# Attention outputs turned in two half-array products, divided on GpSimd, with the instruction order picked from fifteen plans

## The chip, the core and the metric

The kernel runs on one core of a Trainium2 chip. A core has TensorE (PE; its weight loads are shown apart, as PEld), VectorE (DVE), ScalarE (ACT), GpSimd (POOL) and SyncE (SP), which here only issues transfers. Each engine takes its instructions in the order in which they stand in its own queue; semaphores order the engines among each other. The metric is the time of one execution on the device in microseconds (us). Matrix products land in PSUM, which the kernel manages as eight banks of 128 x 512 float32.

## The reference

A stack of two transformer layers over 2048 tokens of 256 features, each an attention with 16 heads of 16 features and a gated feed-forward of width 1024; every part adds the layer norm of its output to its input. Cut to what matters:

```python
scores = einsum('bhqd,bhkd->bhqk', q, k) * scale      # causal mask
probs = softmax(scores)                                # over keys
y = einsum('bhqk,bhkd->bhqd', probs, v)
y = y.transpose(0, 2, 1, 3).reshape(B, T, C)
return y @ W_o.T + b_o
...
x = x + layernorm(attn0(layernorm(x)))
x = x + layernorm(ffn0(layernorm(x)))
x = x + layernorm(attn1(layernorm(x)))
x = x + layernorm(ffn1(layernorm(x)))
```

## The kernel before

**Tiling.** The tokens are cut into four chunks `c` of 512, a chunk into four tiles `t` of 128 rows. The heads form four groups `g` of four. One unit of attention is one query chunk with one group of heads; the list `UNITS` names the 16 of a layer in this order: chunk 0 with groups 0 and 1, chunks 1, 2 and 3 with all four groups, chunk 0 with groups 2 and 3. The keys of a unit run over tiles `kt` up to the end of its own chunk.

**One unit.** First come the maxima: `maxima` multiplies queries by keys (L749, with the mask added by L745), two halves of the array side by side, a bank each, and DVE takes the largest of every row (L757). The rows of maxima are split into three bfloat16 parts on POOL (L787 to L791), turned by four products with the identity over the whole array (L803), and copied by ACT to `mrow` (L807). Then `weighted` runs over the key tiles: PE adds minus the maximum (L835) and the scores (L840) in two banks, again in halves of the array; ACT takes the exponential (L846) into `pt`; on the tiles of the diagonal POOL zeroes what lies above it (L850); PE multiplies by the values (L857), in four groups of columns of the array, and sums up over the key tiles in one bank, `av`. A value row has 17 columns, the last a one, so that the sum of the exponentials comes along.

**The end of a unit,** which the change touches. ACT copies `av` to `o` (L865); `o` has four heads of 32 rows one below another, and tokens along its columns. The four products of `flip` turn it over the whole array, 128 tokens each, into one bank (L870). `divide` takes the reciprocal of the sums (16 columns: four tiles by four heads, L877) and multiplies (256 columns, L879), both on DVE and straight out of the bank, into `yb[c]`, the attention output of the chunk.

**The end of a chunk.** When its last group is done, `mixed` turns `yb[c]` (L531), multiplies by the output weights (L615), adds the bias (L893), and `add_normed` normalizes and adds it to `x`; the power of -1/2 that the norm needs is taken on POOL (L495, L496). The last chunk to close is chunk 0, at the end of the layer's attention, where the feed-forward follows (L1010, then L1017 to L1022, L976).

**What sets the order.** No order of instructions is written out. A `Plan` collects operations (`plan.op`: engine, an assumed duration, what it reads and writes, a rank), and `Plan.run` plays them through with these durations: it looks for the operation that could start first, and among those of the same engine that could start within `near` of it takes the one of lowest rank, plus `waiting` times its delay. In that order the instructions are emitted, and it is fixed from then on. PE operations carry a mode ("row" for halves of the array, "col" for groups of columns, "full"); a change of mode is priced by `SWITCH`. Banks, and rings of buffers, are handed out in the same play. There are four plans: attention and feed-forward of each layer. In all of them `near` and `waiting` are 0.1.

Of the kernel before, what the change touches and what calls it, by code (L numbers as in the profile page):

```python
# [11 lines left out]
F32 = mybir.dt.float32  # L12
# [5 lines left out]
ALU = mybir.AluOpType  # L18
# [5 lines left out]
DH = 16  # L24
# [6 lines left out]
P = 128  # L31
CH = 512
NCHUNK = T // CH
TPC = CH // P
# [30 lines left out]
class Buf:  # L65


    def __init__(self, make, ring=None, banks=0):
        self.make, self.ring, self.banks = make, ring, banks
        self.tile, self.at = None, ()  # L70
        self.users, self.writers, self.readers = [], [], []
        if ring is not None and banks != 1:
            ring.asked.append(self)
# [8 lines left out]
class Ring:  # L82


    def __init__(self, n, ordered=False):
        self.slots, self.at, self.ordered = [None] * n, 0, ordered
        self.asked, self.given = [], 0


class Banks:  # L90

# [1 line left out]


    def __init__(self, n):
        self.slots, self.asked, self.given, self.limit, self.singles = [None] * n, [], 0, 2, 4

    def ready(self, i):

# [12 lines left out]
    def soonest(self, b, others, later):  # L112


        if b.banks == 2 and (self.asked[self.given] is not b or self.pairs() == self.limit):
            return None
        if later and b.banks == 1:
            used = sum(self.ready(i) is None and self.slots[i].banks == 1 for i in range(len(self.slots)))
            if used + others >= self.singles:
                return None  # L120
        free = sorted(t for t, _ in self.choices(b.banks))
        return free[others] if len(free) > others else None

    def give(self, b, now):
        t, i = min((max(t, now), i if b.banks == 2 else -i) for t, i in self.choices(b.banks))
        b.at = range(abs(i), abs(i) + b.banks)
        for i in b.at:
            self.slots[i] = b
        if b.banks == 2:
            self.given += 1  # L130


class Places:
# [2 lines left out]

    def __init__(self, n, left):
        self.slots, self.asked, self.left = [None] * n, [], left

    def choices(self):  # L140

# [22 lines left out]
class Plan:  # L164
# [7 lines left out]
    free, mode = {}, None  # L172
    LAG = {"DVE": 0.08, "ACT": 0.1, "PE": 0.2}

    def __init__(self, near=0.1, waiting=0.1):
        self.ops, self.near, self.waiting = [], near, waiting

    def op(self, engine, us, fn, r=(), w=(), after=(), hold=(), rank=0.0, mode=None, lanes=(0, 1), lag=0.0, load=LOAD):
        bufs = list(dict.fromkeys([*r, *w, *hold]))
# [13 lines left out]
        self.ops.append(o)  # L193
        return o

    def run(self):
        free, mode, waiting = Plan.free, Plan.mode, {}
        ready, after = [], {}
        for o in self.ops:
            waiting[o] = sum(d.end is None for d in o.after)  # L200
            for d in o.after:
                after.setdefault(d, []).append(o)
            if waiting[o] == 0:
                ready.append(o)
        done = 0
        while ready:
            best = []
            pairs = min((o.rank for o in ready if o.pair and o.pair.tile is None), default=math.inf)
            widest = min((o.rank for o in ready if o.wide and o.wide.tile is None), default=math.inf)
            for o in ready:  # L210
                at = max((d.end + self.HOP for d in o.after), default=0.0)
                wanted = {}
                for b in o.bufs:
                    if b.ring is not None and b.tile is None:
                        ring = b.ring
                        if b.banks:
                            soonest = ring.soonest(b, wanted.get(ring, 0), o.rank > (pairs if b.banks < 3 else widest))
                            wanted[ring] = wanted.get(ring, 0) + 1
                            if soonest is None:
                                at = None  # L220
                                break
                            at = max(at, soonest + self.HOP)
                            continue
                        n = wanted.get(ring, 0)
                        wanted[ring] = n + 1
                        if ring.ordered and ring.asked[ring.given + n] is not b:
                            at = None
                            break
                        old = ring.slots[(ring.at + n) % len(ring.slots)]
                        if old is not None:  # L230
                            if any(u.end is None for u in old.users):
                                at = None
                                break
                            at = max(at, max(u.end for u in old.users) + self.HOP)
                if at is None:
                    continue
                if o.engine == "PE":
                    lanes, more = (o.lanes, 0.0) if o.mode == mode else ((0, 1), self.SWITCH[o.mode] + o.load - self.LOAD)
                    at = max([at + o.load] + [free.get(("PE", x), 0.0) + more for x in lanes])
                else:  # L240
                    at = max(at, free.get(o.engine, 0.0))
                best.append((at, o))
            assert best, "nothing can start"
            first = min(best, key=lambda p: p[0])
            at, o = min((p for p in best if p[1].engine == first[1].engine and p[0] <= first[0] + self.near),
                        key=lambda p: (p[1].rank + self.waiting * (p[0] - first[0]), p[0]))
            for b in o.bufs:
                if b.ring is not None and b.tile is None and b.banks:
                    b.ring.give(b, at)
                elif b.ring is not None and b.tile is None:  # L250
                    b.ring.slots[b.ring.at] = b
                    b.ring.at = (b.ring.at + 1) % len(b.ring.slots)
                    b.ring.given += 1
                b.t
            o.fn()
            if o.engine == "PE":
                mode = o.mode
                for x in (0, 1):
                    free["PE", x] = at + o.us if x in o.lanes else max(at, free.get(("PE", x), 0.0))
            else:  # L260
                free[o.engine] = at + o.us
            o.end = at + o.us + o.lag
            done += 1
            ready.remove(o)
            for n in after.get(o, ()):
                waiting[n] -= 1
                if waiting[n] == 0:
                    ready.append(n)
        assert done == len(self.ops)
        Plan.mode = mode  # L270
        self.span = max(o.end for o in self.ops)


@with_exitstack
def kernel(ctx: ExitStack, tc: tile.TileContext, x_in, cols_in, rows_in, wd_in, wuq_in, rot_in,
# [15 lines left out]
    def new(pool, shape, dtype, tag, name, n, ordered=True):  # L291

        ring = rings.setdefault(tag, Ring(n, ordered))
        assert len(ring.slots) == n
        return Buf(lambda: pool.tile(shape, dtype, tag=tag, name=name, bufs=n), ring)

    def bank(name):
        b = Buf(lambda: psum[:, b.at[0], :], banks, 1)
        return b
# [130 lines left out]

    neghalf = const.tile([P, 2 * TPC], F32, tag="neghalf", name="neghalf")
    nc.gpsimd.memset(neghalf, -0.5)
    ident = const.tile([P, P], F32, tag="ident", name="ident")
    make_identity(nc, ident)

# [254 lines left out]
    class Attention:  # L690
# [28 lines left out]
        def over(self, cs):  # L719

            return [o for c in cs for b in self.kb[c] for o in b.readers]

    rpm, rmx = Ring(2), Ring(2)

    def maxima(layer, plan, n, qb, first_rank, span):
# [84 lines left out]
    def attention(layer, plan, wo, wob, bo, scale, tail):  # L810

        L, Vs, kb, vb = layer.L, layer.V, layer.kb, layer.vb
        with tc.tile_pool(name=f"at{L}", bufs=1) as at:
            yb = {}
            for tag in ("Q", "y", "pt", "o"):
                rings.pop(tag, None)

            def weighted(n, c, g, qb, mrow):
# [44 lines left out]
                rk = n + 1.1  # L863
                o = new(at, [P, CH], F32, "o", f"o{L}{n}", 1)
                plan.op("ACT", 0.50, lambda: nc.scalar.copy(o.t, av.t), r=[av], w=[o], rank=rk)  # L865
                s = bank(f"ot{L}{n}")

                def flip():
                    for t in range(TPC):
                        nc.tensor.transpose(s.t[:, t * P:(t + 1) * P], o.t[:, t * P:(t + 1) * P], ident)  # L870

                plan.op("PE", 0.5, flip, r=[o], w=[s], hold=[yb[c]], rank=rk, mode="full")

                def divide():
                    by = s.t.rearrange("p (n e) -> p n e", e=32)
                    r = small.tile([P, 4 * TPC], F32, tag="r", name=f"r{L}{n}", bufs=4)
                    nc.vector.reciprocal(r, by[:, :, DH])  # L877
                    dst = as_tiles(yb[c].t)[:, :, 64 * g:64 * g + 64].rearrange("p t (j d) -> p t j d", j=4)
                    nc.vector.tensor_tensor(  # L879
                        dst, by.rearrange("p (t j) e -> p t j e", j=4)[:, :, :, 0:DH],  # L880
                        r.rearrange("p (t j) -> p t j", j=4).unsqueeze(3).to_broadcast([P, TPC, 4, DH]), ALU.mult)

                plan.op("DVE", 0.7, divide, r=[s], w=[yb[c]], rank=rk)

            def mixed(c, rank):
                yT = transposed(plan, yb[c], f"y{L}{c}", rank)
# [319 lines left out]
```

## Time and profile before

| | |
|---|---|
| median of three runs | 1311.26 us (1307.37 to 1312.85) |
| the profiled execution, its own time | 1308.48 us |
| its span, first to last instruction | 1306.8 us, mean TensorE clock 0.974 |
| instructions | 22980 |
| L757 on DVE, maxima, 1088 instructions | 672.9 us busy |
| L846 on ACT, exponentials, 640 | 546.0 us busy |
| L865 on ACT, copy of `av` to `o`, 32 | 18.9 us busy, 590 ns each |
| L803 on PE, turning rows of maxima, 128 | 12.9 us busy |
| L531 on PE, turning `y`, 64 | 9.2 us busy |

A line of the profile's groups names the line of the kernel, the engine, the operation, what it writes and reads, the size and the count; then the busy time and the mean duration of one; then the time that the engine stood idle before it, and who ended that. Products on PE overlap, so that 128 of 285 ns can have 20.9 us of busy time. The first attention takes about 80 to 556 us of the span, the first feed-forward about 556 to 690, the second attention 690 to 1188, the second feed-forward the rest.

### The profile page before, as it was taken

To read this page: it belongs to the slowest core of one execution; us is meant where nothing else is said; L and a number is where in the kernel's file an instruction comes from. 1 tells how busy PE (TensorE), PEld (TensorE's weight loads), DVE (VectorE), ACT (ScalarE), POOL (GpSimd) and SP (SyncE) were. 2 spreads that over 40 slices of the span, in tenths; PEclk is the share of its full clock that TensorE was granted. 3 is DMA by queue.
4 is the path that set the end of the run, shared out by engine and by line. 5 is a ranking of instruction groups with operands and counts; after the bars stand their busy time and mean duration, and the time that the engine had idled before them with its cause. 6 is when DMAs were issued, how large, how long until landed. Compare 5 with 4: busy or idle time off the path is not lost.

```text
span 1306.8 us, 22980 instructions
## 1 busy us (share of the span) xinstructions
PE 1218.0 (93%) x8888; PEld 680.9 (52%) x8888; DVE 902.3 (69%) x1714; ACT 795.0 (61%) x1100; POOL 333.4 (26%) x640
## 2 busy tenths in 40 slices
PE   4889999999999999889987999999999999997996
PEld 3655545444444443568765455454444443445884
DVE  4588899889978852364445968978898888234432
ACT  3346654776566678666533566557655676885663
POOL 6032111211110112356422212111101200134564
PEclk8899999999999999989997999999999999998998
DMA  5550501500000000000064041040000000000000
GB/s 152 177 178 17 178 17 40 188 17 18 17 1 18 17 1 18 25 9 1 13 211 137 11 153 42 17 146 17 17 17 18 18 1 17 17 1 2 1 33 33
DMA packets 43488, 65.71 MB, mean 50 GB/s; under 512 B 10740, under 2 KB 15441, under 8 KB 43377
## 3 DMA queue, kind: packets, MB, share of 16 engines
q1 hardware_dynamic: 43040, 63.80, 15.8%
q8 instruction: 70, 1.15, 0.4%
q0 software_dynamic: 48, 0.11, 0.1%
q10 hardware_dynamic: 288, 0.31, 0.1%
q14 instruction: 42, 0.34, 0.1%
HBM read 41.14 MB, written 23.07 MB: 49 GB/s over the span
## 4 chain that ended last, share of the span: by engine, by line
PE 70%; DVE 14%; ACT 4%; DMA 3%; issue 3%; POOL 2%; SPq 2%; POOLq 0%; ACTq 0%; DVEq 0%
PE banks L857 17%; DVE pm L757 12%; PE banks L749 10%; PE banks L835 10%; PE banks L840 8%; PE banks L1010 8%; PE banks L615 7%; PE banks L976 4%; PE banks L745 3%; ACT pt L846 3%; PE banks L531 1%; DMA sc_q<-wide 1%; ACT wide L506 1%; PE banks L870 1%; SPq L567 1%
## 5 line engine op out<-in xcount | busy, mean ns | idle before, releaser
L757 DVE TENSOR_REDUCE pm<-banks 128x1 f32<-128x512 f32 (+1 forms) x1088 | 672.9, 684 | 155.4 <-PE banks L749 150.0
L846 ACT ACTIVATE pt<-banks 128x1024 f32<-128x1024 f32 (+3 forms) x640 | 546.0, 898 | 262.4 <-PE banks L840 242.1
L840 PE MATMUL banks<-Q,K 64*128 64x512 f32 (+3 forms) x1248 | 319.1, 519 | 0.0
L749 PE MATMUL banks<-K,Q 64*128 64x128 f32 (+2 forms) x1728 | 305.1, 359 | 11.1 <-DMA Q<-sc_q 4.9
L857 PE MATMUL banks<-pt,V 128*32 128x512 f32 (+3 forms) x2560 | 303.7, 546 | 1.9 <-POOL pt L850 1.0
L835 PE MATMUL banks<-mrow,sel 64*128 64x512 bf16 (+3 forms) x1280 | 247.5, 354 | 13.0 <-ACT pt L846 8.8
L749 PEld LDWEIGHTS banks<-K,Q 64*128 64x128 f32 x1728 | 193.7, 186 | 111.3 <-DVE pm L757 61.7
L835 PEld LDWEIGHTS <-sel 64*128 64x128 bf16 x1280 | 78.4, 93 | 232.5 <-issue 218.7
L850 POOL TENSOR_SCALAR_AFFINE_SELECT pt<-pt 128x256 f32<-128x256 f32 x256 | 102.7, 406 | 335.5 <-ACT pt L846 332.9
L1010 PE MATMUL banks<-F,F 128*128 128x512 f32 x512 | 134.5, 407 | 5.2 <-DVE wide L557 5.2
L840 PEld LDWEIGHTS banks<-Q,K 64*128 64x128 f32 x1248 | 135.3, 195 | 4.5 <-issue 3.7
L1010 PEld LDWEIGHTS banks<-F,F 128*128 128x128 f32 x512 | 99.2, 196 | 27.3 <-DVE wide L557 5.7
L1019 DVE SCALAR_TENSOR_TENSOR fu<-banks,cols,sl 128x512 f32<-128x512 f32 x64 | 47.4, 750 | 74.3 <-ACT sl L1017 33.1
L857 PEld LDWEIGHTS banks<-pt,V 128*32 128x32 f32 x2560 | 53.0, 108 | 86.5 <-issue 65.5
L1022 POOL TENSOR_TENSOR fl<-fu,fh 128x512 fp32r<-128x512 f32 x64 | 81.7, 1288 | 61.4 <-ACT fh L1021 61.1
L787 POOL TENSOR_SCALAR mx<-best 128x16 bf16<-128x16 f32 x32 | 9.8, 308 | 314.5 <-DVE best L782 314.5
L745 PE MATMUL banks<-mask,half 64*128 64x512 bf16 x256 | 67.3, 388 | 0.3 <-DVE pm L757 0.3
L1021 ACT CAST fh<-fu 128x512 fp32r<-128x512 f32 x64 | 39.5, 621 | 38.6 <-DVE fu L1019 37.2
L976 PE MATMUL banks<-fh,F 128*128 128x512 f32 x128 | 53.0, 414 | 6.6 <-DVE fu L1019 6.6
L976 PE MATMUL banks<-fl,F 128*128 128x512 f32 x128 | 52.3, 408 | 4.4 <-POOL fl L1022 4.4
L1017 ACT ACTIVATE sl<-banks,cols 128x512 f32<-128x512 f32 x64 | 43.5, 689 | 13.7 <-PE banks L1010 13.3
L549 POOL TENSOR_TENSOR x<-x,wide 128x1024 f32<-128x1024 f32 x16 | 37.9, 2371 | 35.0 <-ACT wide L506 35.0
(122 smaller groups left out, 934.1 us busy)
## 6 DMA issues: line engine op xcount, KB each, us to landing
K<-sc_k SPq DMA_DIRECT2D x128, 128.0 KB
Q<-sc_q SPq DMA_DIRECT2D x120, 128.0 KB
sc_q<-wide SPq DMA_DIRECT2D x48, 256.0 KB
sc_k<-wide SPq DMA_DIRECT2D x32, 256.0 KB
x<-in_x_dram SPq DMA_DIRECT2D x4, 512.0 KB
out_dram<-x SPq DMA_DIRECT2D x4, 512.0 KB
f<-in_ffn_dram SPq DMA_DIRECT2D x2, 768.0 KB
F<-sc_q SPq DMA_DIRECT2D x8, 128.0 KB
```

What stands on the lines that cost most here:

```text
L615: nc.tensor.matmul(s.t[:, at:at + n], a, b, start=start, stop=stop)
L745: nc.tensor.matmul(s.t.rearrange("p (d k) -> p d k", k=P), half16[b, x, :], mask_qk[b, x, :, :], start=x == 0, stop=False)
L749: nc.tensor.matmul(s.t[:, to:to + k], qb.t[b, i, t * P:(t + 1) * P], layer.K(kc)[b, 2 * g + i, k0:k0 + k], start=not masked, stop=not mask ...
L757: nc.vector.tensor_reduce(dst, src, AX.X, ALU.max)
L835: nc.tensor.matmul(s.t[:, e, 0:nq], sel[b:b + 64, i, :], mrow.t[b:b + 64, off:CH], start=True, stop=False)
L840: nc.tensor.matmul(s.t[:, e, 0:nq], layer.K(kt // TPC)[b:b + 64, 2 * g + i, k * P:(k + 1) * P], qb.t[b:b + 64, i, off:CH], start=False, st ...
L846: plan.op("ACT", 0.1 + nq / 620, lambda s=s, pt=pt, nq=nq: nc.scalar.activation(pt.t[:, :, 0:nq], s.t[:, :, 0:nq], AF.Exp, scale=scale), r ...
L850: plan.op("POOL", 0.41, lambda pt=pt: nc.gpsimd.affine_select(out=pt.t[:, :, 0:P], in_=pt.t[:, :, 0:P], compare_op=ALU.is_ge, fill=0.0, ba ...
L857: nc.tensor.matmul(av.t[32 * j:32 * j + 32, off:CH], Vs[kt // TPC][:, kt % TPC, DV * h:DV * h + 32], pts[kt, j // 2].t[:, j % 2, 0:nq], st ...
L976: nc.tensor.matmul(dn[dh].t, wdn[:, fc, dh * P:(dh + 1) * P], halves[fc][j].t, start=fc == 0 and j == 0, stop=fc == 7 and j == 1)
L1010: nc.tensor.matmul(s.t[:, i, :], w[:, cc, fc * P:(fc + 1) * P], xT[j].t[:, cc, :], start=n == 0, stop=n == 3)
L1022: plan.op("POOL", 1.3, lambda fu=fu, fh=fh, fl=fl: nc.gpsimd.tensor_tensor(fl.t, fu.t, fh.t.bitcast(F32), ALU.subtract), r=[fu, fh], w=[fl ...
```

## The change

Three things are changed.

1. The output of a unit is turned by a new function, `turned`: for each half `e` of the rows of `o` (two heads, 64 rows) four products with the 64 x 64 identity, into a bank of its own, in mode "row"; and one ACT copy of 256 columns out of each bank into `ot` in SBUF. Eight smaller products and two copies stand where four products stood.
2. The division runs on POOL and reads `ot`: the reciprocal is a power of -1 over 16 columns (`minus1` is a new constant), followed by the multiplication over 256 columns. The plan is given 1.1 us for both.
3. `Plan.run` plays each plan fifteen times, with five values of `near` and three of `waiting`, keeps the pair whose play ends first, and emits that one. The bookkeeping of buffers in the play is rewritten for it (`given`, and `soonest` and `give` of `Ring`) so that a play can be taken back. For this program the four plans take (near, waiting) = (0.05, 0.05), (0.05, 0.05), (0.14, 0.1) and (0.17, 0.05).

The turning of the rows of maxima in `maxima` (L803) is not touched.

```diff
-    def __init__(self, near=0.1, waiting=0.1):
-        self.ops, self.near, self.waiting = [], near, waiting
+    NEAR, WAITING = (0.05, 0.08, 0.11, 0.14, 0.17), (0.05, 0.1, 0.2)
+
+    def __init__(self):
+        self.ops = []
...
-    def run(self):
-        free, mode, waiting = Plan.free, Plan.mode, {}
+    def order(self, near, waiting, emit=False):
...
-            at, o = min((p for p in best if p[1].engine == first[1].engine and p[0] <= first[0] + self.near),
-                        key=lambda p: (p[1].rank + self.waiting * (p[0] - first[0]), p[0]))
+            at, o = min((p for p in best if p[1].engine == first[1].engine and p[0] <= first[0] + near),
+                        key=lambda p: (p[1].rank + waiting * (p[0] - first[0]), p[0]))
...
+    def run(self):
+
+        tried = [(self.order(near, waiting), near, waiting) for near in self.NEAR for waiting in self.WAITING]
+        self.span = self.order(*min(tried)[1:], emit=True)
...
+    minus1 = const.tile([P, TPC, 4, 1], F32, tag="minus1", name="minus1")
+    nc.gpsimd.memset(minus1, -1.0)
...
+    def turned(plan, src, dst, r, w, name, rank):
+
+        for e in range(2):
+            s = bank(f"{name}{e}")
+
+            def flip(s=s, e=e):
+                b = slice(64 * e, 64 * e + 64)
+                for t in range(TPC):
+                    nc.tensor.transpose(s.t[:, t * 64:t * 64 + 64], src(t, b), ident[b, b])
+
+            plan.op("PE", 0.45, flip, r=[r], w=[s], hold=[w], rank=rank, mode="row", lanes=(e,))
+            plan.op("ACT", 0.33, lambda s=s, e=e: nc.scalar.copy(dst(e), s.t[:, 0:TPC * 64].rearrange("p (t q) -> p t q", t=TPC)),
+                    r=[s], w=[w], rank=rank)
...
-                s = bank(f"ot{L}{n}")
-
-                def flip():
-                    for t in range(TPC):
-                        nc.tensor.transpose(s.t[:, t * P:(t + 1) * P], o.t[:, t * P:(t + 1) * P], ident)
-
-                plan.op("PE", 0.5, flip, r=[o], w=[s], hold=[yb[c]], rank=rk, mode="full")
+                ot = new(at, [P, TPC, P], F32, "ot", f"ot{L}{n}", 1)
+                turned(plan, lambda t, b: o.t[b, t * P:(t + 1) * P], lambda e: ot.t[:, :, 64 * e:64 * e + 64], o, ot, f"ot{L}{n}", rk)
 
                 def divide():
-                    by = s.t.rearrange("p (n e) -> p n e", e=32)
-                    r = small.tile([P, 4 * TPC], F32, tag="r", name=f"r{L}{n}", bufs=4)
-                    nc.vector.reciprocal(r, by[:, :, DH])
+                    by = ot.t.rearrange("p t (j e) -> p t j e", e=32)
+                    r = small.tile([P, TPC, 4, 1], F32, tag="r", name=f"r{L}{n}", bufs=4)
+                    nc.gpsimd.tensor_tensor(r, by[:, :, :, DH:DV], minus1, ALU.pow)
                     dst = as_tiles(yb[c].t)[:, :, 64 * g:64 * g + 64].rearrange("p t (j d) -> p t j d", j=4)
-                    nc.vector.tensor_tensor(
-                        dst, by.rearrange("p (t j) e -> p t j e", j=4)[:, :, :, 0:DH],
-                        r.rearrange("p (t j) -> p t j", j=4).unsqueeze(3).to_broadcast([P, TPC, 4, DH]), ALU.mult)
-
-                plan.op("DVE", 0.7, divide, r=[s], w=[yb[c]], rank=rk)
+                    nc.gpsimd.tensor_tensor(dst, by[:, :, :, 0:DH], r.to_broadcast([P, TPC, 4, DH]), ALU.mult)
+
+                plan.op("POOL", 1.1, divide, r=[ot], w=[yb[c]], hold=[yb[c]], rank=rk)
```

## The prediction

> **What bounds the kernel now.** I read the busy shares first, then the same shares by stretch, then the chain of work that ended last, and last the rows of what the change touches. The busy times of the page:
>
> ```profile
> PE 1218.0 (93%) x8888; PEld 680.9 (52%) x8888; DVE 902.3 (69%) x1714; ACT 795.0 (61%) x1100; POOL 333.4 (26%) x640
> PE 70%; DVE 14%; ACT 4%; DMA 3%; issue 3%; POOL 2%; SPq 2%; POOLq 0%; ACTq 0%; DVEq 0%
> ```
>
> The second line is the chain's share by engine: PE carries the end, DVE sometimes takes over, POOL hardly appears. By stretch (PE, PEld, DVE, ACT and POOL busy, clock, DMA), inside the first attention:
>
> ```profile
> 160.00:300.00 140.00, 137.21 (x1117) 68.16 (x1113) 124.45 (x221) 89.54 (x111) 22.79 (x58) 1.00 0.21 65
> 420.00:520.00 100.00, 98.40 (x826) 41.16 (x822) 59.57 (x101) 75.46 (x88) 13.76 (x36) 1.00 0.04 12
> ```
>
> PE is busy 98% in both; beside it DVE has 89% in the early units and ACT 75% in the late ones. POOL has 14 to 16%, at full clock. So a microsecond off PE counts nearly whole, one off DVE in part, one added to ACT little, and one added to POOL nothing unless somebody waits for that instruction. The rows for what is removed or added (mean ns after the count):
>
> ```profile
> L870 PE MATMUL banks<-ident,o 128*128 128x128 f32 x128 | 20.9, 285 | 0.9
> L877 DVE RECIPROCAL r<-banks 128x16 f32<-128x16 f32 x32 | 8.1, 252 | 15.2 <-PE banks L870 13.7 <-ACT pt L846 1.5
> L879 DVE TENSOR_TENSOR y<-banks,r 128x256 f32<-128x256 f32 x32 | 13.6, 425 | 1.1
> L846 ACT ACTIVATE pt<-banks 128x256 f32<-128x256 f32 x64 | 23.0, 386 | 37.5 <-PE banks L840 28.3 <-POOL pt L850 5.0 <-issue 3.5
> L496 POOL TENSOR_TENSOR rs_ya<-ve_ya,neghalf 128x4 f32<-128x4 f32 x8 | 8.3, 1042 | 0.7
> L788 POOL TENSOR_TENSOR rest<-best,mx 128x16 f32<-128x16 f32 x32 | 7.1, 221 | 2.7
> L1022 POOL TENSOR_TENSOR fl<-fu,fh 128x512 fp32r<-128x512 f32 x64 | 81.7, 1288 | 61.4 <-ACT fh L1021 61.1 <-PE banks L1010 0.3
> L549 POOL TENSOR_TENSOR x<-x,wide 128x1024 f32<-128x1024 f32 x16 | 37.9, 2371 | 35.0 <-ACT wide L506 35.0
> ```
>
> The reader is to see one thing above all: L496 is a power of 4 columns and takes 1042 ns; L788 is an addition of 16 columns and takes 221. On POOL a power is not priced like an addition.
>
> **PE, the flips (32 units of head group and query chunk).** In the timeline a flip looks like this:
>
> ```profile
> 322.53 0.18 PEld L749 LDWEIGHTS banks<-K,Q 64*128 64x128 f32 x1 [0.41 <-DVE pm L757]
> 322.95 0.42 PEld L870 LDWEIGHTS banks<-ident,o 128*128 128x128 f32 x4 [0.24 <-ACT pt L846]
> 323.54 0.16 PEld L857 LDWEIGHTS banks<-pt,V 128*32 128x32 f32 x8 [0.17 <-issue]
> ```
>
> The 0.42 us from the last L749 to the first L870 repeats: it is the median of the 21 places where L749 stands before L870, while L749 to a following score product (L835) is 0.16: before it enters the full array PE stands some 0.26 us. The four products start 0.109 apart, and the exit to a score product is 0.205. So a flip between two half-array products takes 0.42 + 3 x 0.109 + 0.205 = 0.95, less the 0.16 that would be there anyway: 0.79 us. After the change each flip is eight products of 64 rows. Nearest row: the eight L749 products 64x128 in two halves, whose first and last start are 0.40 us apart (57 ns each, the two halves side by side). So 0.45 us instead of 0.79: 0.34 saved. Ends: if the loads of the two halves queue at 0.109 each, 0.87 and thus 0.1 lost; if 64 moving columns halve it, 0.55 saved. The built program's order has 28 of 32 flips wholly between half-array products, and entries into full-array mode fall from 81 to 55. 27 x 0.34 = **9 us saved**, ends -15 and +3. Rows of maxima (L803, also full-array, four products each) keep their form: the change's short description names them too, but that half is not in the diff.
>
> **DVE.** Removed: 32 x (252 + 425 ns) = 21.7 us. DVE is on the chain 14% of the time (3 us) and stands at 89% beside a PE that waits for its banks in the early units; I take a third, **7 us saved**, ends 3 and 21.7.
>
> **ACT.** Two copies of 128x256 out of PSUM per unit, priced by the 386 ns row of that size: 32 x 0.77 = 25 us, at 61% busy. In the late units it delays exponentials. With ACT's 4% of the chain it is 1 us, with one in six 4; I take **4 us lost**, ends 0 and 12. Each flip now holds two banks until these copies, where it held one until DVE's division; it is inside these ends.
>
> **POOL, the division.** The multiplication 128x256: from L1022 and L549 the slope is (2371 - 1288) / 512 = 2.1 ns per column and the intercept 0.2, so 0.75 us (estimate from these rows). The reciprocal as a power over 16 columns was never run: if the 1042 ns are fixed, 1.04; if the excess over an addition (1042 - 205 - 8 = 829 ns) goes with columns, 0.2 + 16 x 0.209 = 3.5 us. A rule of the Trainium skill (GPSIMD Engine Reference, section When to use GPSIMD) speaks against the move, but mildly: elementwise work belongs on VectorE, GpSimd takes about twice as long with two inputs. By it the division is estimated at 2 x 0.68 = 1.4 us, near the 1.1 that the planner is given. The row says 1.8 to 4.3. I take 4.3: the planner's own price of the two small instructions at L495/L496 is written as 0.3 + 0.2 per column, the same slope as 0.209. POOL gains 32 x 4.3 = 137 us of work, which fits into its 970 idle; what counts is who waits:
>
> - 24 inner units (chunks 1 to 3, less closings): in POOL's timeline the next instruction after a flip at 322.95 begins at 344.63, and elsewhere 8 to 25 us later. Hidden, 0.
> - Closings: yb of a chunk is turned (L531) after its last group. In the new order four closings in mid-attention have 2.1 to 2.5 us of PE work between flip and y flip. Needed: 0.45 for the flip, 0.2 until readable, 0.77 + half an exponential (0.5) for ACT, 0.1, 4.3 = 6.3 against 0.45 + 2.4: PE, whose queue is in order, stands 3.5 us; four times 14.
> - The two ends of attention: chunk 0 closes and the feed-forward's products stand behind it. Before, in the chain:
>
> ```profile
> 1188.45 0.44 PE banks L870 x4
> 1188.89 1.17 PE banks L1010 x5
> 1190.05 0.45 PE banks L531 x4
> ```
>
>  The wait is covered by L1010. After, one L1010 product stands between: 6.3 - 0.45 - 0.23 = 5.6 us each, 11. Together 25, of which I let a fifth be caught up by engines that run ahead: **20 us lost**. With the rule's 1.4 us it would be 4 x 0.6 + 2 x 2.7 = 8, less a fifth: 6.
> - Chunk 0's units mask every key tile, so L850 stands directly behind the division (0.3 to 0.7 us behind the flip in the trace at units 0, 13 and 14 of each layer). Each then comes up to 4 us later; weighted values and everything behind them in PE's queue wait, with some 2 to 3 us of products as cover: 6 x 1.3 = **8 us lost**, ends 0 and 15; 1 by the rule.
>
> **The order.** Each of the four plans is now drawn up fifteen times and the one of least planned span is emitted; it picks (0.05, 0.05), (0.05, 0.05), (0.14, 0.1) and (0.17, 0.05) where (0.1, 0.1) stood. Loads of K and Q on SP's queue change places too, all ahead of use and with 5% DMA share late. No row prices this: between -13 and +10 us, taken as 0. It chooses with the division at 1.1 us, so the covers above are cut to a price which I doubt.
>
> **Sum** by the row: -9 - 7 + 4 + 20 + 8 = +16. By the rule: -9 - 7 + 4 + 6 + 1 = -5. The profiled execution took 1308.48 us (span 1306.8); the median of the runs shown is 1311.26, 2.8 above. 1308.5 + 16 = 1324.5, and I say **1324**.
>
> **Rivals.** *Slower by the power* (the forecast), 0.52: 1324, own range 1314 to 1338; its weak point is that no power over 16 columns was run. It decides where the division on POOL takes over about 2.7 us (half-way between 1.4 and 4.3 the sum passes +5). *Faster*, 0.29: the power costs about the same for 4 and 16 columns, flips save 0.45 us each, and DVE proves to be the brake in the units with 89%, so that half of its relief counts: -12 - 11 + 4 + 6 + 1 = -12, thus 1296, own range 1288 to 1304. For it: the loads of L749 wait 62.7 us for DVE's L757 in the list of waits; against: PE at 98%. *Wash*, 0.13: the division is hidden but so is the gain, 1308 (-5 + 2 of order). *The new order is worse on the chip*, 0.06, whatever the division takes: +12, 1323. [...]
>
> Change smaller than 0.5% (6.6 us) cannot be told from none. Slower by more: 0.42 of the first and all of the last but a little, 0.05, and some of the wash: 0.52, and I give 0.55; same 0.15; faster 0.30. The range 1296 to 1336 leaves about one in ten at each side.
>
> **What would show it.** The power row on POOL at 128x16: 3.5 us right, 1.0 wrong. The multiplication 0.75. PE idle ahead of the turning of y (L531 in the lines of before) at the closings, with POOL's y as the releaser, some 3.5 us each; DVE busy 880, ACT 820, POOL 470. Flips: about 57 ns per product, no 0.42 ahead. If the power takes 1 us and the closings do not stand, the forecast falls and the time is under 1305.

## The result, and the profile after

| | before | after |
|---|---|---|
| median | 1310.97 us (1307.37 to 1312.85, 4 runs) | 1325.41 us (1325.16 to 1327.84, 4 runs) |
| ratio to before, 95% interval | | 1.012 [1.0102, 1.0138] |
| the profiled execution, its own time | 1308.48 us | 1325.32 us |
| its span, mean TensorE clock | 1306.8 us, 0.974 | 1323.6 us, 0.967 |

The changed kernel is 14.4 us slower. The forecast was 1324, by the way that it named the likeliest. New lines are the half flips (L750), their copies (L753), the power (L905) and the multiplication (L907). The others have moved because code was added above them: the turning of `y` is L550 (before L531), the output weights L634 (L615), the mask L883 (L850), the weighted values L890 (L857), maxima L782 and L790 (L749 and L757), the feed-forward's first product L1036 (L1010).

The same two lines of the page of the kernel after, busy times and the chain's shares by engine:

```profile
PE 1220.0 (92%) x9016; PEld 687.4 (52%) x9016; DVE 884.8 (67%) x1650; ACT 809.3 (61%) x1164; POOL 446.8 (34%) x705
PE 68%; DVE 13%; POOL 6%; ACT 5%; issue 3%; DMA 3%; SPq 2%; POOLq 0%; ACTq 0%; DVEq 0%
```

POOL was 2% of the chain and is now 6%: an engine that is idle two thirds of the time has come into the way. PE's busy time has hardly changed (1218.0 before), while the span of the profiled execution grew by 16.8 us: PE stands more. The rows of what was added, by shape (mean ns after the count, then the idle time of the engine before them and who ended it):

```profile
L905 POOL TENSOR_TENSOR r<-ot,minus 128x16 f32<-128x16 f32 x32 | 93.6, 2926 | 150.5 <-ACT ot L753 150.1
L907 POOL TENSOR_TENSOR y<-ot,r 128x256 f32<-128x256 f32 x32 | 19.9, 621 | 2.5
L753 ACT COPY ot<-banks 128x256 f32<-128x256 f32 x64 | 21.8, 395 | 6.7 <-PE banks L750 6.7
L750 PE MATMUL banks<-ident,o 64*128 64x64 f32 x256 | 21.6, 230 | 2.0 <-DVE pm L790 0.5 <-ACT pt L879 0.3 <-DVE wide L671 0.2
L550 PEld LDWEIGHTS banks<-ident,y 128*128 128x128 f32 x64 | 7.1, 146 | 17.4 <-POOL y L907 12.0 <-DVE pm L790 3.0 <-ACT pt L879 1.3
```

The power takes 2926 ns and the multiplication 621: 3.55 us per unit, where DVE took 0.68. And the last line shows who waits for it: the loads for turning `y` stood 12.0 us behind POOL's `y`. The list of waits has that again (total, times, longest), and the masks beside it:

```profile
PEld banks L890 <- POOL pt L883: 14.0, 28, 3.4
PEld banks L550 <- POOL y L907: 12.0, 6, 3.4
PE banks L890 <- POOL pt L883: 6.2, 3, 3.3
```

Before, the first of these was smaller, and in place of the second there was only a short wait for DVE, which divided then:

```profile
PEld banks L857 <- POOL pt L850: 8.2, 27, 1.2
PEld banks L531 <- DVE y L879: 0.8, 2, 0.4
```

The timeline of PE's loads has the six stands one by one (start, length, and in brackets the time that it stood before and for whom):

```profile
226.37 0.42 PEld L550 LDWEIGHTS banks<-ident,y 128*128 128x128 f32 x4 [0.37 <-POOL y L907]
...
560.35 0.72 PEld L550 LDWEIGHTS banks<-ident,y 128*128 128x128 f32 x4 [3.38 <-POOL y L907]
...
853.38 0.42 PEld L550 LDWEIGHTS banks<-ident,y 128*128 128x128 f32 x4 [1.23 <-POOL y L907]
...
1008.20 0.42 PEld L550 LDWEIGHTS banks<-ident,y 128*128 128x128 f32 x4 [1.43 <-POOL y L907]
...
1177.44 0.47 PEld L550 LDWEIGHTS banks<-ident,y 128*128 128x128 f32 x4 [2.25 <-POOL y L907]
...
1207.23 0.42 PEld L550 LDWEIGHTS banks<-ident,y 128*128 128x128 f32 x4 [3.38 <-POOL y L907]
```

Four are closings in mid-attention, with 0.4 to 2.3 us (the other two of the six there show no stand behind POOL); those at 560 and 1207 are the two ends of attention, with 3.4 each. Here is the last one, as the chain of waits tells it (start, length, what):

```profile
1202.09 0.47 PE banks L750 x8
1202.55 0.30 issue
1202.85 0.66 ACT ot L753 x2
1203.51 0.07 issue
1203.58 2.91 POOL r L905
1206.49 0.07 issue
1206.56 0.63 POOL y L907
1207.19 0.04 issue
1207.24 0.65 PE banks L550 x4
1207.89 0.43 PE banks L634 x2
1208.33 0.63 PE banks L1036 x2
1208.95 4.54 PE banks L634 x14
```

From the end of the flip (1202.55) to the turning of `y` (1207.24) the chain leaves PE for 4.69 us, of which the power is 2.91. The last line shows a second price: fourteen products of the output weights take 4.54 us here. In the same place before, the chain had

```profile
1192.14 3.04 PE banks L615 x14
```

The stretches (length, busy PE, PEld, DVE, ACT, POOL, granted clock) say why; the first two are those shown of before, inside the first attention, the other two the stand and what follows it:

```profile
160.00:300.00 140.00, 135.81 (x1104) 68.22 (x1101) 115.27 (x202) 87.81 (x116) 41.02 (x69) 0.99 0.20 61
420.00:520.00 100.00, 99.23 (x854) 45.44 (x850) 66.17 (x109) 75.43 (x91) 23.94 (x42) 1.00 0.04 12
1203.00:1208.50 5.50, 2.15 (x13) 1.65 (x13) 0.00 (x0) 1.66 (x4) 3.52 (x2) 1.00 0.00 1
1208.50:1212.00 3.50, 3.50 (x10) 2.81 (x9) 0.38 (x1) 1.98 (x3) 0.00 (x0) 0.52 0.00 0
```

Inner attention is not where the loss is: PE is as full there as before, and DVE's share in the early units has come down from 89 to 82%. After this stand, however, PE runs 3.5 us at half clock.

### The profile page after: what moved, and what is told of

Its sections match the earlier page's. It is cut to its first block, busy times and chain, and to the rows that moved or that the text cites. A ratio compares the mean times of both kernels' runs of the same rounds, so it can differ in the third digit from the quotient of the medians.

```text
span 1323.6 us, 23337 instructions
## 1 busy us (share of the span) xinstructions
PE 1220.0 (92%) x9016; PEld 687.4 (52%) x9016; DVE 884.8 (67%) x1650; ACT 809.3 (61%) x1164; POOL 446.8 (34%) x705
## 4 chain that ended last, share of the span: by engine, by line
PE 68%; DVE 13%; POOL 6%; ACT 5%; issue 3%; DMA 3%; SPq 2%; POOLq 0%; ACTq 0%; DVEq 0%
PE banks L890 17%; DVE pm L790 11%; PE banks L782 10%; PE banks L868 10%; PE banks L873 8%; PE banks L634 7%; PE banks L1036 7%; PE banks L1002 3%; ACT pt L879 3%; PE banks L778 3%; POOL r L905 2%; PE banks L550 1%; ACT wide L525 1%; SPq L586 1%; POOL fl L1048 1%
## 5 line engine op out<-in xcount | busy, mean ns | idle before, releaser
L790 DVE TENSOR_REDUCE pm<-banks 128x1 f32<-128x512 f32 (+1 forms) x1088 | 672.8, 681 | 175.0 <-PE banks L782 172.3
L782 PE MATMUL banks<-K,Q 64*128 64x128 f32 (+2 forms) x1728 | 309.7, 360 | 10.2 <-DMA Q<-sc_q 6.3
L890 PE MATMUL banks<-pt,V 128*32 128x512 f32 (+3 forms) x2560 | 304.3, 545 | 7.9 <-POOL pt L883 6.2
L782 PEld LDWEIGHTS banks<-K,Q 64*128 64x128 f32 x1728 | 197.4, 189 | 85.0 <-DVE pm L790 43.2
L883 POOL TENSOR_SCALAR_AFFINE_SELECT pt<-pt 128x256 f32<-128x256 f32 x256 | 102.4, 406 | 241.4 <-ACT pt L879 239.3
L905 POOL TENSOR_TENSOR r<-ot,minus 128x16 f32<-128x16 f32 x32 | 93.6, 2926 | 150.5 <-ACT ot L753 150.1
L1036 PE MATMUL banks<-F,F 128*128 128x512 f32 x512 | 131.6, 401 | 0.8 <-DVE fu L1045 0.8
L1036 PEld LDWEIGHTS banks<-F,F 128*128 128x128 f32 x512 | 97.0, 191 | 22.0 <-DVE fu L1045 1.2
L890 PEld LDWEIGHTS banks<-pt,V 128*32 128x32 f32 x2560 | 51.9, 108 | 93.5 <-issue 64.8
```

What stands on the lines that cost most here:

```text
L782: nc.tensor.matmul(s.t[:, to:to + k], qb.t[b, i, t * P:(t + 1) * P], layer.K(kc)[b, 2 * g + i, k0:k0 + k], start=not masked, stop=not mask ...
L790: nc.vector.tensor_reduce(dst, src, AX.X, ALU.max)
L883: plan.op("POOL", 0.41, lambda pt=pt: nc.gpsimd.affine_select(out=pt.t[:, :, 0:P], in_=pt.t[:, :, 0:P], compare_op=ALU.is_ge, fill=0.0, ba ...
L890: nc.tensor.matmul(av.t[32 * j:32 * j + 32, off:CH], Vs[kt // TPC][:, kt % TPC, DV * h:DV * h + 32], pts[kt, j // 2].t[:, j % 2, 0:nq], st ...
L905: nc.gpsimd.tensor_tensor(r, by[:, :, :, DH:DV], minus1, ALU.pow)
L1036: nc.tensor.matmul(s.t[:, i, :], w[:, cc, fc * P:(fc + 1) * P], xT[j].t[:, cc, :], start=n == 0, stop=n == 3)
```

## The experiments

My theory: the power on POOL makes the division late at closings and ahead of masks, and PE, whose queue is in order, stands there. Rivals: the half flips with their copies and second bank cost the time; or the new order does, whatever the division takes. Each kernel was timed beside the kernel before (1310.4 to 1311.1 us there); the ratios are to that. "To the letter" below means that `plan.op` is told the same as in the kernel that it is compared with, so that the order of instructions on PE and ACT stays as it was.

### Parts of the change alone

**Division back on DVE**, everything else kept, with the plan told so:

```diff
-  nc.gpsimd.tensor_tensor(r, by[:, :, :, DH:DV], minus1, ALU.pow)
+  nc.vector.reciprocal(r, by[:, :, :, DH:DV])
-  nc.gpsimd.tensor_tensor(dst, ...)
+  nc.vector.tensor_tensor(dst, ...)
-  plan.op("POOL", 1.1, divide, ...)
+  plan.op("DVE", 0.7, divide, ...)
```

> The changed kernel with one part undone: reciprocal and multiplication of the outputs run on VectorE again, now out of the copy in SBUF; the half-array flips, the two copies and the fifteen plans stay. If the division's time in GpSimd's queue behind the closings, the ends and the masks is the cause: 1309 us, from 1303 to 1313. If the new order of instructions is the cause, or the two ScalarE copies and the second bank: 1320 to 1326, no change to the changed kernel.

Measured: 1301.01 us (1300.49 to 1304.49), ratio 0.9934 [0.9918, 0.9949]. 24.4 us below the changed kernel, and below the range that I gave. The division is the loss, and the rest of the change is worth about 9 us, more than either theory gave it. The order is another one here too; the series in one order below separates that.

**The order alone**: the kernel before, with the fifteen plans.

```diff
-  ot = new(at, [P, TPC, P], ...); turned(plan, ...)
+  s = bank(f"ot{L}{n}"); plan.op("PE", 0.5, flip, r=[o], w=[s], ..., mode="full")
-  plan.op("POOL", 1.1, divide, r=[ot], ...)
+  plan.op("DVE", 0.7, divide, r=[s], ...)
```

> The kernel before with the fifteen plans alone; flip over the whole array, division on VectorE out of PSUM. My theory gives the order no part in the loss: 1311 us, from 1305 to 1316. If the order is the cause: 1320 or more.

Measured: 1301.5 us (1300.0 to 1305.08), ratio 0.9936 [0.992, 0.9952]. A miss: the search brings 9 us by itself, and I had put it at nothing. Beside it, the kernel with the division back on DVE shows no gain from the flips: 1301.0 against 1301.5, each in its own order.

**No search**: flips and division as changed, one pair of values.

```diff
-  NEAR, WAITING = (0.05, 0.08, 0.11, 0.14, 0.17), (0.05, 0.1, 0.2)
+  NEAR, WAITING = (0.1,), (0.1,)
```

> The changed kernel with the one pair (0.1, 0.1) of before in place of fifteen: half-array flips and division on GpSimd alone. My theory: as slow as the changed kernel, 1325 us, from 1318 to 1332. If the order is the cause: 1311.

Measured: 1332.14 us (1328.93 to 1335.78), ratio 1.0167 [1.0145, 1.0188]. The search is worth 7 us here too. It hid a third of what the other two parts lose: some 21 us without it, 14 with it.

### The division, unit by unit, in one order

An order drawn anew for each variant moves everything. In the next four kernels the changed kernel's order is kept to the letter, and only the engine that divides is chosen by the number `n` of the unit in `UNITS`:

```diff
+  on_dve = ...
+  if on_dve: nc.vector.reciprocal(r, ...)
+  else: nc.gpsimd.tensor_tensor(r, ..., minus1, ALU.pow)
+  (nc.vector if on_dve else nc.gpsimd).tensor_tensor(dst, ...)
```

**All on DVE** (`True`):

> The changed kernel with its order of instructions kept to the letter (same planner, same prices, same picks); only the engine of the division is VectorE in all 32 units. So the order can't differ. If the division's stay on GpSimd is the cause, this is 1303 us, from 1300 to 1308, and PE no longer waits for y. If the order drawn for the changed kernel is what is bad and the first experiment was fast because its order was another: 1318 or more.

Measured: 1311.2 us (1308.83 to 1314.14), ratio 1.0008 [0.9996, 1.0021]. A miss: between the two cases that I had put down. In one order the division on POOL costs 14.2 us. That is below the 24.4 of the first experiment; the 10 us between the two kernels with the same work come with the order alone, here one drawn without the divisions on DVE, there one drawn with them.

**GpSimd in the inner units alone** (`n in (0, 1, 5, 9, 13, 14, 15)` on DVE):

> The same fixed order; VectorE divides in the units that close a chunk (5, 9, 13, 15) and in those next to masks of chunk 0 (0, 1, 14), GpSimd in the other nine of each layer. The prediction says that these inner units hide the division wholly: no slower than with VectorE everywhere, or up to 3 us faster, as VectorE is relieved of 12 us: 1299 to 1306. If GpSimd's division costs in every unit: 9/16 of the loss, 1313 or more.

Measured: 1305.11 us (1304.24 to 1307.87), ratio 0.9961 [0.9947, 0.9975]. As expected, the slow division is hidden in the nine inner units of a layer. Taking it off DVE gains 6.1 us in this order, twice the most that I had expected; the order reckons with no division on DVE. Its chain at the last closing:

```profile
1186.45 0.40 PE banks L750 x8
1186.85 0.43 PE banks L1040
1187.28 0.02 issue
1187.30 0.66 PE banks L550 x4
...
1190.00 3.08 PE banks L634 x14
```

Flip, one feed-forward product, turning of `y`: no stand, and the fourteen products take 3.08 us again.

**GpSimd in the closing units alone** (`n not in (5, 9, 13, 15)` on DVE):

> The same fixed order; GpSimd divides only in the four units of a layer that close a chunk (5, 9, 13, 15), VectorE in all others. The prediction put 20 us on these eight places: 1321 us, from 1316 to 1326. If the closings are a small part and the masks behind the division the larger: 1308 to 1312.

Measured: 1323.39 us (1322.03 to 1325.31), ratio 1.0099 [1.0082, 1.0117]. Eight of 32 divisions carry +12.2 us, nearly the whole loss. Its waits, in which L911 is the multiplication:

```profile
PEld banks L550 <- POOL y L911: 13.0, 6, 3.4
PEld banks L890 <- POOL pt L883: 8.7, 24, 1.3
```

The six stands are there, 13.0 us where the changed kernel has 12.0, and the masks' row has nearly its old size. With all divisions on DVE there is no wait of L550 for POOL, and on the masks there is

```profile
PEld banks L890 <- POOL pt L883: 8.0, 25, 0.9
PE banks L890 <- POOL pt L883: 0.4, 1, 0.4
```

**GpSimd in units 0, 1 and 14 alone**, the units of chunk 0 that close nothing:

> The changed kernel's order to the letter, with GpSimd dividing only in units 0, 1 and 14 of each layer: chunk-0 units that close no chunk and whose successor's masks stand behind the division. All other units divide on DVE. Same arithmetic. The split of the changed kernel's 14.2 us over the all-DVE version into closings (+12.2), inner units (-6.1) and these units (+8.1) has its last term by difference only. If it is additive: 1311.2 + 8.1 = 1319 (1316 to 1322). If the difference came from how the parts act together (a late mask behind a closing, or a gain of the inner units that the closings undo): 1311 to 1315, and the last term is no cost of these units alone.

Measured: 1316.41 us (1312.91 to 1317.67), ratio 1.0034 [1.0022, 1.0046]: +5.2 over all on DVE. Its waits:

```profile
PEld banks L890 <- POOL pt L883: 13.0, 29, 3.4
PE banks L890 <- POOL pt L883: 5.5, 3, 3.2
```

Against 8.0 and 0.4 in the version with all on DVE: 5 us more on masks (the second row shows the longest of the same stands at the products), which is the time lost. The prediction named units 0, 13 and 14; 13 closes a chunk and is in the run before this one, where the masks' row hardly grew (8.7). So the three groups alone give +12.2 - 6.1 + 5.2 = 11.3 of the 14.2; the other 2.9 arise only where they are together (in the changed kernel's chain a division begins only after a residual addition on POOL, at 1193.71, and the mask behind it only at 1197.28), or are within what such medians differ by.

### What the power itself costs

**The reciprocal on DVE, the multiplication on POOL**, in all units, the plan told so:

```diff
+  plan.op("DVE", 0.25, reciprocal, r=[ot], w=[rr], ...)
-  plan.op("POOL", 1.1, divide, r=[ot], ...)
+  plan.op("POOL", 0.7, multiply, r=[ot, rr], ...)
```

> The changed kernel with the power alone replaced: the reciprocal of 16 columns is VectorE's, the multiplication stays on GpSimd in all units (priced 0.25 and 0.7). If the length of the power is what makes GpSimd's division late: 1301 us, from 1297 to 1307. If it is the hand-over to GpSimd and its queue, whatever the length: 1315 or more.

Measured: 1303.81 us (1300.21 to 1308.21), ratio 0.9942 [0.9923, 0.9962]. The rows of its two parts:

```profile
L903 DVE RECIPROCAL rr<-ot 128x16 f32<-128x16 f32 x32 | 7.9, 246 | 16.5 <-ACT ot L753 16.4
L909 POOL TENSOR_TENSOR y<-ot,rr 128x256 f32<-128x256 f32 x32 | 19.9, 622 | 153.3 <-DVE rr L903 153.3
```

One more hand-over between engines, and POOL still has the multiplication in every closing; yet 21.6 us of the 24.4 are back, and PE's loads wait 0.6 us in all for POOL's `y`. So POOL's taking part is not what costs. The order is its own here, so that not all of the 21.6 is the power's length by itself.

### Telling the plan the truth

**The true price**: `plan.op("POOL", 3.7, divide, ...)` instead of 1.1.

> The changed kernel with one number different: the plan is told that the division takes 3.7 us on GpSimd (measured 2.93 + 0.62 and a gap) instead of 1.1. If the cause is that PE's fixed order turns y too early for the division, the planner now puts work in between in mid-attention, while the ends cannot be covered: 1316 us, from 1311 to 1320. If the queue itself or the flips are the cause: 1322 to 1328.

Measured: 1324.6 us (1317.16 to 1325.42), ratio 1.0105 [1.0087, 1.0123]. A miss. In its trace only the two ends still wait for POOL's `y` (8.4 us in 2 stands), and the masks' row is down to 6.3 us; the time came back elsewhere in an order that differs everywhere. Its profiled execution is the fastest of its runs, at 1317.16 and a granted clock of 0.971, so the trace does not stand for the median: the other four, at 1321.8 to 1325.4, had 0.962 to 0.964. Time times the share of clock not granted is 38 us in the first and 48 to 50 in the others (estimate from these figures), so that a good part of the 7 us can be clock; that is not shown.

**The split of the inner-units kernel, with true prices** (0.7 on DVE, 3.7 on POOL):

> Half-array flips, fifteen plans, GpSimd dividing in nine inner units of each layer and VectorE in units 0, 1, 5, 9, 13, 14, 15, and the plan told so with 3.7 and 0.7 us. The division's place is the cause, so with the order drawn for it this is the best of the family: 1297 us, from 1293 to 1302. If GpSimd's division costs where nobody waits for it: 1305 or more.

Measured: 1305.14 us (1302.62 to 1308.08), ratio 0.9953 [0.9939, 0.9968]. A miss again: no better than the same split in an order drawn for a wrong price (1305.11), though all on DVE gained 10 us from its own order. So with each in its own order the split is 4 us slower than all on DVE (1301.0): the 6.1 us of the inner units are a gain in one order, not in general.

### What the flips bring

**Half flips without copies**: DVE divides each half straight from its bank.

```diff
-  turned(plan, ...)                              # two flips, two ACT copies
-  plan.op("POOL", 1.1, divide, r=[ot], ...)
+  for e in range(2):
+      plan.op("PE", 0.45, flip, r=[o], w=[s], ..., mode="row", lanes=(e,))
+      plan.op("DVE", 0.5, divide, r=[s], w=[yb[c]], ...)
```

> Fifteen plans and half-array flips, without the ScalarE copies: VectorE divides straight out of the two banks, in two halves (four small instructions instead of two), own order. If the flips save 9 us on PE and the copies gave it back: 1293 us, from 1289 to 1298, against 1301 for the order alone. If PE's saved time isn't on the path there: 1300 to 1305, for VectorE has some 10 us more to do.

Measured: 1300.75 us (1299.3 to 1303.4), ratio 0.9929 [0.991, 0.9947]. As without half flips (1301.5). What it pays with is in its rows:

```profile
L912 DVE RECIPROCAL r<-banks 128x8 f32<-128x8 f32 x64 | 12.8, 200 | 13.9 <-PE banks L905 13.7 <-issue 0.2
L914 DVE TENSOR_TENSOR y<-banks,r 128x128 f32<-128x128 f32 x64 | 18.7, 292 | 2.2
```

31.5 us on DVE where the whole division took 21.7 before: half the columns do not cost half the time (200 against 252 ns, 292 against 425).

**Each whole-array flip done twice**, in the order of the order-alone kernel to the letter:

```diff
-  for t in range(TPC):
+  for t in (*range(TPC), *range(TPC)):
```

> The kernel with the order alone, in the same order to the letter (the plan isn't told); each whole-array flip is made twice, so TensorE has 32 x 4 x 0.109 = 14 us more work in the places of the flips. If TensorE's time there is on the path, as the prediction had it when it put 9 us on the shorter flips: 1315 us, from 1311 to 1319. If it is hidden there, which would explain that shorter flips brought nothing: 1301 to 1305.

Measured: 1310.9 us (1310.11 to 1313.84), ratio 1.0005 [0.9995, 1.0015]. The flips' rows, first of the order alone, then with each done twice:

```profile
L903 PE MATMUL banks<-ident,o 128*128 128x128 f32 x128 | 20.8, 285 | 3.5 <-ACT o L898 1.7 <-ACT pt L879 0.8
```

```profile
L903 PE MATMUL banks<-ident,o 128*128 128x128 f32 x256 | 34.7, 279 | 3.5 <-ACT o L898 1.7 <-ACT pt L879 0.8
```

13.9 us more on PE at this place made 9.4 us of time: two thirds counts. At two thirds, the 11 us that the forecast's 0.33 per flip would save are worth about 7 (estimate). Neither version with half flips shows them. A part may never have been saved: without copies, PE's busy time is 1211.4 us against 1216.0 in the order alone, 4.6 less. The rest may have gone to DVE's 10 us more in the version without copies, and in the one with copies to ACT's 21 us (64 copies of 0.39 us in parallel with much else) or to the second bank. These were not separated.

## Why the prediction was right, point by point

The direction and the mechanism came true: the power makes the division late, and PE stands at closings and ahead of masks. That the time did so within 1.4 us is luck: several steps were off by more than that, with both signs, and the sum began at the profiled execution's 1308.5 us (from the median of 1311.0 the same +16 would have given 1327). All differences below are of medians.

| step of the sum | forecast | shown |
|---|---|---|
| half flips, less their copies | -9 + 4 | -0.5 (division back on DVE, against the order alone) |
| DVE's relief | -7 (all units) | -6.1 (the 18 inner units alone, one order) |
| closings and ends | +20 | +12.2 (closing units, one order) |
| masks behind the division | +8 | +5.2, up to 8.1 together with the rest |
| the order | 0 | -8.9 from the search in the kernel before; +10.2 because the order is drawn for another division |

The right column, with the 8.1, adds up to 15.0 against 14.4 measured. That is no evidence: the runs lead step by step from the kernel before to the changed one and the 8.1 is their remainder, so that they must add up, but for the 0.6 by which the kernel before differed between the two timings (1310.4 and 1311.0).

- **The power.** The choice between the row and the rule decided the forecast, and the row was right. I took 3.5 us for 16 columns; it takes 2.93, and the multiplication 0.62 where I had 0.75. The slope was too steep because I gave all but an addition's time to the columns: 1042 ns for 4 and 2926 for 16 make 157 ns per column and 0.41 us fixed. 3.55 instead of 4.3 us is still above the 2.7 from which I said that the division decides. Busy times came out as DVE 885, ACT 809 and POOL 447 us, where I had 880, 820 and 470. The rule of the Trainium skill that I weighed (GPSIMD Engine Reference, When to use GPSIMD: about twice as long with two inputs) is too dear for the multiplication, 621 ns against 426 to 474 for the same operands on DVE (all on DVE in one order, and in its own), and too cheap for this pair by far: 2926 against 249 ns for a reciprocal of 16 columns. It speaks of sums and products, not of powers.
- **Closings and ends.** Number and releaser are as forecast: four in mid-attention and two ends. The size is not: 0.4 to 2.3 us where I had 3.5, and 3.4 where I had 5.6, 12.0 us in all against 25 (20 after the fifth that I let be caught up). This term, 20 where the closing units cost 12.2, was the most oversized. At the last end the flip's end and the turning of `y` lie 4.69 us apart where I had 5.85: 0.75 of the difference is the division's price, the rest mostly the half exponential that I put ahead of ACT's copies. They came 0.30 us after the flip.
- **Inner units.** They hide the division, as said. That -6.1 is near the forecast's -7 is luck: I had let a third of the 21.7 us of all units count, and here half of the 12.2 us of 18 units did, in one order. I wrote 24 inner units; there are nine in a layer, 18. Since each costs nothing, the sum did not feel it.
- **Flips.** A flip with its entry and exit falls from a median of 1.1 us to 0.77, so 0.33 us as forecast (0.34), but only where its eight products stand together, which is so in less than half of the 32. In the others the order has spread them among other products, and the first and the last start 0.3 to 2.5 us apart. That the products take not 57 but some 35 ns each changes little. What failed is the step from one flip to the time: not all flips save so much, PE's time counts two thirds, and what is left does not show beside the copies and the second bank.
- **The order.** This term was mis-sized. I had its bounds (-13 to +10) and took 0; a gain and a loss near these bounds occurred at once and nearly cancelled, which is luck too. The search brings 8.9 us in the kernel before and 6.7 in the changed one. An order drawn for a division of 1.1 us on POOL gives 10 back when DVE divides, against one drawn for that; whether an order drawn for 3.55 us could regain it is what the true price was to show, and didn't.
- **Rivals.** *Faster* fell with the power's row, *wash* with the 12.2 us of the closings. The *worse order on the chip* is refuted as it was meant: the search makes both the old and the new work faster. But a redrawn order moves this kernel by 10 us either way with the same work, more than most terms of my sum.

No version beats the order alone for certain: division on DVE with half flips (1301.0), half flips without copies (1300.8) and the order alone (1301.5) cannot be told apart, and these three are some 9 us faster than the kernel before.

## What to carry to other kernels

Before work is moved to an idle engine, find its operation by name in the trace and scale it by columns; an operation next to it on the same engine can differ tenfold (an addition of 16 columns 221 ns, the power 2926). Then ask not how idle the engine is but which few of its instructions somebody waits for: here, in one order, 8 divisions of 32 lost twice what the 18 inner ones gained. When a planner draws the order, test a part in the old order to the letter as well as in its own, or the redrawing will be taken for the part.

## What the runs showed that I had not expected

**A stand can cost twice.** After the last closing's stand the granted clock fell to 0.52 for 3.5 us, and the fourteen products took 4.54 us instead of 3.04. Without the stand, in the kernel with GpSimd in inner units only, the same stretch has full clock:

```profile
1190.00:1193.10 3.10, 3.10 (x16) 2.74 (x15) 0.69 (x1) 1.72 (x2) 0.00 (x0) 1.00 0.00 0
```

This is what the Trainium skill says (TensorE: Matmul & The Clock Gate, Part 1: The HAM clock gate): after a window of about 3.4 us that counts as idle the clock is halved until a busy one has passed. But PE was not idle for a whole window: in the 3.4 us before the clock fell (1205.05 to 1208.46) it was busy for 1.22 us, so thin work was enough. It did not happen at every stand. The clock was half for 3.4 us from 559.9 and from 1177.7 too, and stayed full after the stands at 853 and 1008; at 226 it had been half just before. Half-clock stretches are not new either: the kernel before has one from 1184.0, for 3.4 us.

**How much of the differences is clock?** Time times the share of clock not granted, as the median of a kernel's executions, is 39 us in the kernel before and 43.7 in the changed one. In the one-order series it is 40.6 with all divisions on DVE, 39.6 with the closings on POOL (37 to 48 in its five executions) and 36.5 with the inner units on POOL. So the 12.2 us of the closings are not clock by this measure, while a part of the inner units' 6.1 can be. All on DVE in its own order has 33.8. Among executions of the same kernel, 1 us more of this went with about half a us of time (a line through the 140 on record, each measured from its kernel's mean). By that, some 3 of the 10 us between the two orders with all on DVE can be clock, and 2 of the inner units' gain; these are estimates, and no run changed the clock by itself.
